# A ring of five equal x tiles, one more block loaded over GpSimd's queue, and left-over rows cut by fields, in a pairwise bilinear kernel

## Chip, cores and metric

One core of one Trainium2 chip. The metric is the device time of one execution, in microseconds. Times of a kernel are medians of its runs in the fast state; on one core the runs of one kernel here agree within about 0.3%. The profile's own span is some 1.8 us shorter than the timed run that it was taken from.

## The reference

For each of 4096 rows there are 32 fields of 64 values. For each of the 496 pairs i < j, field i is multiplied by that pair's 64 x 64 matrix, and the product is multiplied elementwise by field j. All is float32. The output has 4096 x 496 x 64 values, 520 MB; inputs are 34 MB of x and 8 MB of W.

```python
idx_i, idx_j = np.triu_indices(F, k=1)
vi = inputs[:, idx_i, :]
vj = inputs[:, idx_j, :]
vidots = jnp.einsum('bpd,pde->bpe', vi, W)
return vidots * vj
```

## The kernel before

The rows are cut into 16 blocks of 256, each of two tiles of 128 partitions, so 32 tiles of work of some 40 us each. W stays in SBUF. Per tile, PE (TensorE) transposes x and multiplies it with W, and VectorE (DVE in the views; with ACT, which is ScalarE, and GpSimd for some products) multiplies by field j into one of three output buffers. Each tile is written in four stores of about 4 MB, all from SyncE's queue.

Blocks 0 and 1 are loaded at the start. The others come in pairs, in seven **events**: at step 4 of the last tile of a pair, the next pair is loaded. The even block goes over ACT's queue, the odd one over GpSimd's, in a special shape: 120 rows, a tiny transfer, then the 8 rows that are left. The 120 rows leave one of the 16 DMA engines out. The tiny transfers are meant to keep that engine the same from event to event. The records don't show how; what was measured is that other row counts in two such transfers, before the first event and after the last, cost 30 us (1359.92 us, "Another engine left out").

```python
xb = const.tile([P, 5 * FD + 3 * GAP], F32, tag="xb", name="xb")
...
starts = [0, FD + GAP, 2 * FD + GAP, 3 * FD + GAP, 4 * FD + 2 * GAP]

def slot_of(blk: int):
    e, second = divmod(blk, 2)
    return ((1, 3), (2, 0))[e % 2][second]
...
SWR = 120

def turn_engines(k: int):
    n = k if k > 1 else 17
    c = used[0] % 8
    used[0] += 1
    src = x[: NB * n].rearrange("(p k) f d -> p k f d", k=NB)
    tc.keep_in_program_order(
        nc.gpsimd.dma_start(out=scratch[:n, :, c : c + 1], in_=src[:, :, 0, 0:1])
    )

def load_fifteen(blk: int):
    rows = rows_of(x, blk).rearrange("(p k) f d -> p k f d", k=NB)
    dst = x_block(blk)

    def part(ps: slice, ks: slice):
        tc.keep_in_program_order(nc.gpsimd.dma_start(out=dst[ps, ks], in_=rows[ps, ks]))

    part(slice(0, SWR), slice(0, NB))
    turn_engines(1)
    for k in range(NB):
        part(slice(SWR, P), slice(k, k + 1))
...
LATE = 4
loads = {place[2 * NB * e - 1, LATE]: 2 * e for e in range(1, NBLK // 2)}
...
turn_engines(5)              # before the loop over the steps
for s, (t, st) in enumerate(sched):
    if s in loads:
        load_fifteen(loads[s] + 1)
    if s - 3 in loads:
        tc.keep_in_program_order(load_x(loads[s - 3], nc.scalar))
    ...                      # transposes, two matmuls, the product
    if pa + m in ends:       # a group of pairs is complete
        nc.sync.dma_start(out=..., in_=ot[...])
turn_engines(11)             # after the loop
```

The gap in the x buffer keeps the two halves of GpSimd's blocks apart, so that they move in 8 KB packets (1792 of 8192 bytes on q0, by the packet records) rather than merged ones of 16 KB, as ACT's blocks do, which lie together (896 of 16,384 bytes on q10).

## Time and profile before

| what | value |
|---|---|
| time, median of 3 runs | 1334.1 us (1333.88 to 1335.71) |
| bytes moved, mean rate | 563 MB, 422 GB/s |
| DMA packet time, four queues | 99.3% of 16 engines' span |
| PE, VectorE busy | 86%, 71% |
| lone DMA engine at the end | about 7 us |

The four queues in the page are q1 (SyncE's: stores and first loads), q0 (GpSimd's), q10 (ACT's) and q8 (instructions). A digit in the row "DMA" says how busy the 16 engines were in a slice of the span, in tenths, and the row GB/s below it says what they moved. The two differ when packets are slow: an engine counts as busy while a packet is under way, however long it takes (1122 to 1130 us in the changed kernel: share 0.99 at 252 GB/s). The prediction shows the lines.

### The profile page before, as it was taken

How to read it: one execution, taken by the hardware profiler on the slowest of the kernel's cores; microseconds unless marked ns; L12 is line 12 of the kernel's file. 1: busy time of each engine (PE TensorE's matmuls, PEld its weight loads, DVE VectorE, ACT ScalarE, POOL GpSimd, SP SyncE). 2: the span in 40 equal slices, each digit the busy share in tenths (PEclk: the TensorE clock that was granted, in tenths of full speed). 3: DMA queues.
4: the chain of work that ended last, by engine and by line, in shares of the span. 5: the costliest groups of instructions: out<-in, count | busy, mean ns of one | idle time of the engine just before them, and what ended most of it. 6: DMA issues, size and time to landing. Idle time of an engine off the chain costs nothing.

```text
span 1333.2 us, 17377 instructions
## 1 busy us (share of the span) xinstructions
PE 1146.3 (86%) x6644; PEld 597.9 (45%) x6644; DVE 952.0 (71%) x1287; ACT 471.6 (35%) x627; POOL 558.5 (42%) x264
## 2 busy tenths in 40 slices
PE   6989989996989979998888888888888988888983
PEld 3555444443444434444444444444444444444441
DVE  5778767875777757777667776777767776677773
ACT  4553423333333323333233332343333332333330
POOL 1862524435434434344344352444434444334440
PEclk9999989998999989999899998999989999899997
DMA  9999999999999999999999999999999999999997
GB/s 389 431 430 429 381 428 433 429 433 422 428 431 434 426 423 431 430 431 428 420 435 428 434 411 426 428 433 430 422 425 437 424 430 403 428 433 430 424 426 307
DMA packets 24306, 563.16 MB, mean 422 GB/s; under 512 B 3232, under 2 KB 3232, under 8 KB 3360
## 3 DMA queue, kind: packets, MB, share of 16 engines
q1 hardware_dynamic: 20576, 532.69, 93.5%
q0 software_dynamic: 2640, 14.70, 2.8%
q10 hardware_dynamic: 1008, 14.68, 2.8%
q8 instruction: 52, 0.85, 0.2%
q14 instruction: 30, 0.25, 0.0%
HBM read 41.94 MB, written 520.09 MB: 422 GB/s over the span
## 4 chain that ended last, share of the span: by engine, by line
DMA 48%; PE 25%; DVE 11%; issue 8%; POOL 4%; ACT 3%; DVEq 0%; SPq 0%; ACTq 0%; POOLq 0%
DMA out_dram<-ob 47%; PE ps L298 22%; DVE ob L314 11%; POOL ob L312 3%; ACT ob L311 2%; PE ptx L200 2%; DMA xb<-in_r_inputs_dram 1%; PE ptw L191 1%; POOL xb L152 0%; DVE ob L181 0%; POOL scratch L144 0%; POOL ob L181 0%; DVEq L314 0%; ACT xtb L202 0%; ACT xtb L204 0%
## 5 line engine op out<-in xcount | busy, mean ns | idle before, releaser
L314 DVE TENSOR_TENSOR ob<-ps,xb 128x1024 f32<-128x1024 f32 (+4 forms) x1277 | 939.8, 793 | 347.9 <-DMA out_dram<-ob 173.8
L298 PE MATMUL ps<-wT,xtb 64*128 64x512 f32 (+15 forms) x5760 | 1015.4, 490 | 145.9 <-DVE ob L314 72.5
L312 POOL TENSOR_TENSOR ob<-ob,xb 128x1024 f32<-128x1024 f32 x224 | 529.1, 2367 | 744.6 <-ACT ob L311 717.3
L298 PEld LDWEIGHTS ps<-wT,xtb 64*128 64x128 f32 x5760 | 507.6, 195 | 619.2 <-DVE ob L314 257.1
L311 ACT COPY ob<-ps 128x1024 f32<-128x1024 f32 x224 | 226.8, 1013 | 485.9 <-PE ps L298 342.5
L202 ACT COPY xtb<-ptx 128x512 f32<-128x512 f32 x122 | 71.5, 586 | 311.4 <-PE ptx L200 309.7
L200 PE MATMUL ptx<-ident,xb 128*128 128x128 f32 x512 | 86.2, 292 | 10.8 <-DMA xb<-in_r_inputs_dram 7.1
L200 PEld LDWEIGHTS ptx<-ident,xb 128*128 128x128 f32 x512 | 55.1, 144 | 61.9 <-issue 37.5
L204 ACT COPY xtb<-ptx 64x512 f32<-64x512 f32 x122 | 71.0, 582 | 3.0
L203 ACT COPY xtb<-ptx 64x512 f32<-64x512 f32 x122 | 70.4, 577 | 2.9
L298 PE MATMUL ps<-wT,xb 64*128 64x512 f32 (+15 forms) x244 | 42.5, 465 | 3.4 <-DVE ob L314 1.6
L298 PEld LDWEIGHTS ps<-wT,xb 64*128 64x128 f32 x244 | 20.2, 185 | 21.3 <-DVE ob L314 9.4
L191 PE MATMUL ptw<-ident,ob 128*128 128x128 f32 (+1 forms) x128 | 18.1, 294 | 6.0 <-DVE ob L181 5.8
L191 PEld LDWEIGHTS ptw<-ident,ob 128*128 128x128 f32 (+1 forms) x128 | 15.1, 154 | 12.0 <-DVE ob L181 5.2
L192 ACT COPY wT<-ptw 128x1024 f32<-128x1024 f32 (+1 forms) x15 | 14.9, 992 | 10.1 <-PE ptw L191 10.0
L181 DVE COPY ob<-wT 128x1024 f32<-128x1024 f32 (+1 forms) x7 | 9.5, 1382 | 10.5 <-DMA wT<-in_L_rec_W_dram 10.5
L152 POOL DMA_DIRECT2D xb<-in_r_inputs_dram x21 | 13.3, 636 | 0.0
L202 ACT COPY xb<-ptx 128x512 f32<-128x512 f32 x6 | 3.5, 586 | 18.1 <-PE ptx L200 18.1
L144 POOL DMA_DIRECT2D scratch<-in_r_inputs_dram x9 | 8.4, 934 | 0.3 <-issue 0.3
L181 POOL COPY ob<-wT 128x1024 f32<-128x1024 f32 x4 | 8.0, 2004 | 0.0
L181 ACT COPY ob<-ob 128x1024 f32<-128x1024 f32 x2 | 4.1, 2028 | 0.0
L204 ACT COPY xb<-ptx 64x512 f32<-64x512 f32 x6 | 3.5, 583 | 0.1
(11 smaller groups left out, 11.3 us busy)
## 6 DMA issues: line engine op xcount, KB each, us to landing
out_dram<-ob SPq DMA_DIRECT2D x29, 4064.0 KB, 19.5
out_dram<-ob SPq DMA_DIRECT2D x29, 4032.0 KB, 19.9
out_dram<-ob SPq DMA_DIRECT2D x29, 4000.0 KB, 19.8
out_dram<-ob SPq DMA_DIRECT2D x29, 3776.0 KB, 20.2
xb<-in_r_inputs_dram ACTq DMA_DIRECT2D x7, 2048.0 KB, 22.5
xb<-in_r_inputs_dram POOLq DMA_DIRECT2D x7, 1920.0 KB, 33.7
out_dram<-ob SPq DMA_DIRECT2D x3, 2912.0 KB, 12.6
out_dram<-ob SPq DMA_DIRECT2D x3, 2624.0 KB, 11.2
```

Of the source, the lines that this page charges most:

```text
L152: tc.keep_in_program_order(nc.gpsimd.dma_start(out=dst[ps, ks], in_=rows[ps, ks]))
L181: ins = copy(rp[:r], src[:, k * EU : (k + 1) * EU])
L191: nc.tensor.transpose(pt[:, n, :r], rp[:r, n].rearrange("p h d -> p (h d)"), ident[:r, :r])
L192: copy(wT[:, a:b, k * EU : (k + 1) * EU], pt[:, :, :r].rearrange("p e r -> p r e"))
L200: nc.tensor.transpose(pt[:, u, :], x_tile(t)[:, f : f + 2, :].rearrange("p f d -> p (f d)"), ident)
L202: copy(xT[:, 0], pt)
L203: copy(xT[D:, 1], pt[:D])
L204: copy(xT[:D, 1], pt[D:])
L298: nc.tensor.matmul(ps[:, h, :m, :], xT[t, i // RUN][h * D : (h + 1) * D, (i + h) % 2, i % RUN // 2, :], wT[h * D : (h + 1) * D, pa : pa + ...
L311: nc.scalar.copy(dst, src)
L312: nc.gpsimd.tensor_mul(dst, dst, xj)
L314: nc.vector.tensor_mul(dst, src, xj)
```

## The change

Its intent is to take work away from the one DMA engine that is late. In the last event both blocks go over GpSimd's queue, whose large transfers leave one engine out. For that, any two tiles of the ring must be able to hold a block and still not be neighbours; so the gaps go, the ring has five equal tiles, and a table says which two of them a block takes. The 8 left rows of a block are cut into halves of the fields, each over both tiles, instead of tile by tile. The whole diff:

```diff
--- before.py
+++ after.py
@@ -68,8 +68,7 @@
 
     wT = const.tile([P, NP, E2], F32, tag="wT", name="wT")
     FD = F * D
-    GAP = 16
-    xb = const.tile([P, 5 * FD + 3 * GAP], F32, tag="xb", name="xb")
+    xb = const.tile([P, 5, FD], F32, tag="xb", name="xb")
     XT = 2 * (RUN // 2) * P
     xtb = const.tile([P, 2 * XT], F32, tag="xtb", name="xtb")
     ob = const.tile([P, 3 * cap1, D], F32, tag="ob", name="ob")
@@ -92,29 +91,34 @@
         n = xt_used[0]
         xt_used[0] += 1
         n = n % 4 if t < LEAD else n % 2
-        mem, o = (xtb, n * XT) if n < 2 else (xb, (n - 2) * XT)
+        mem, o = (xtb, n * XT) if n < 2 else (xb[:, 0], (n - 2) * XT)
         return mem[:, o : o + XT].rearrange("p (s u b) -> p s u b", s=2, b=P)
 
 
 
 
 
-    starts = [0, FD + GAP, 2 * FD + GAP, 3 * FD + GAP, 4 * FD + 2 * GAP]
-
-    def slot_of(blk: int):
+    fifteen = (3, 5, 7, 9, 11, 13, 14, 15)
+
+    def slots_of(blk: int):
         e, second = divmod(blk, 2)
-        return ((1, 3), (2, 0))[e % 2][second]
+        if e == 0:
+            return ((1, 2), (3, 4))[second]
+        if e % 2 == 0:
+            return ((2, 3), (1, 4))[second]
+        if 2 * e in fifteen:
+            return ((1, 3), (2, 0))[second]
+        return ((1, 2), (3, 0))[second]
 
     def tile_of(t: int):
 
         blk, k = divmod(t, NB)
-        return blk, 1 - k if slot_of(blk) == 0 else k
+        a, b = slots_of(blk)
+        return blk, k if a < b else 1 - k
 
     def x_block(blk: int):
-        o = starts[slot_of(blk)]
-        step = starts[slot_of(blk) + 1] - o
-        wide = xb[:, o : o + NB * step].rearrange("p (k n) -> p k n", k=NB)
-        return wide[:, :, :FD].rearrange("p k (f d) -> p k f d", d=D)
+        a, b = sorted(slots_of(blk))
+        return xb[:, a : b + 1 : b - a].rearrange("p k (f d) -> p k f d", d=D)
 
     def x_tile(t: int):
         blk, k = tile_of(t)
@@ -148,13 +152,13 @@
         rows = rows_of(x, blk).rearrange("(p k) f d -> p k f d", k=NB)
         dst = x_block(blk)
 
-        def part(ps: slice, ks: slice):
-            tc.keep_in_program_order(nc.gpsimd.dma_start(out=dst[ps, ks], in_=rows[ps, ks]))
-
-        part(slice(0, SWR), slice(0, NB))
+        def part(ps: slice, fs: slice):
+            tc.keep_in_program_order(nc.gpsimd.dma_start(out=dst[ps, :, fs], in_=rows[ps, :, fs]))
+
+        part(slice(0, SWR), slice(0, F))
         turn_engines(1)
-        for k in range(NB):
-            part(slice(SWR, P), slice(k, k + 1))
+        for h in range(2):
+            part(slice(SWR, P), slice(h * F // 2, (h + 1) * F // 2))
 
 
 
@@ -275,8 +279,10 @@
         blk, kt = tile_of(t)
         g, i, c0, m = steps[t][st]
         if s in loads:
-            load_fifteen(loads[s] + 1)
-        if s - 3 in loads:
+            for b in (loads[s], loads[s] + 1):
+                if b in fifteen:
+                    load_fifteen(b)
+        if s - 3 in loads and loads[s - 3] not in fifteen:
             tc.keep_in_program_order(load_x(loads[s - 3], nc.scalar))
         for what, *args in due.get(s, ()):
             if what == "x":
```

## The prediction

> **What bounds the kernel now.** I read the page first, then the DMA view, then windows at the end of the span, then the timeline around the last load. The page's slices of the span, its GB/s row, and three queue rows:
>
> ```profile
> DMA  9999999999999999999999999999999999999997
> GB/s 389 431 430 429 381 428 433 429 433 422 428 431 434 426 423 431 430 431 428 420 435 428 434 411 426 428 433 430 422 425 437 424 430 403 428 433 430 424 426 307
> ...
> q1 hardware_dynamic: 20576, 532.69, 93.5%
> q0 software_dynamic: 2640, 14.70, 2.8%
> q10 hardware_dynamic: 1008, 14.68, 2.8%
> q8 instruction: 52, 0.85, 0.2%
> ```
>
> The 16 DMA engines are busy in every slice but the last, at some 430 GB/s. The queues' shares (93.5, 2.8, 2.8, 0.2) add to 99.3% of 1333.2 us. PE is busy 86% and DVE 71%: compute is close behind, but DMA sets the time. So the time is one engine's packet time plus what engines idle at either end. The end is uneven. From the windows there (columns: span, length, busy time of PE, PEld, DVE, ACT, POOL, clock, DMA share, GB/s):
>
> ```profile
> 1312.00:1322.00 10.00, 0.31 (x4) 0.20 (x4) 0.77 (x4) 0.00 (x0) 0.00 (x0) 0.68 0.98 420
> 1322.00:1324.00 2.00, 0.00 (x0) 0.00 (x0) 0.00 (x0) 0.00 (x0) 0.00 (x0) 0.50 0.75 323
> 1324.00:1326.00 2.00, 0.00 (x0) 0.00 (x0) 0.00 (x0) 0.00 (x0) 0.00 (x0) 0.50 0.08 32
> 1326.00:1328.00 2.00, 0.00 (x0) 0.00 (x0) 0.00 (x0) 0.00 (x0) 0.00 (x0) 0.50 0.04 16
> ```
>
> And the DMA view of 1325.5 to 1331.5:
>
> ```profile
> DMA packets 5, 0.16 MB, mean 27 GB/s; under 512 B 0, under 2 KB 0, under 8 KB 0
> ```
>
> 27 GB/s is one sixteenth of 432. Fifteen engines are done at about 1324 to 1325 and **one engine works alone** for some 7 us, on five stores' packets of 1.19 us each. The trace's packet records show how it got there. In each 4 MB store (128 packets, eight per engine) I took the end of the last packet less that of the ninth from last: a measure of how late the slowest engine is. It is 1.1 to 2 us up to 450 us, 6.2 us just before the last load at 1116 us, 4.1 to 5.2 us just after it, and 7.0 us at the end. It grows steadily between loads and falls after each.
>
> [...] the instruction queue has 52 packets for 0.85 MB, 16 KB each. If they go to one engine, they are 52 x 0.61 us (a 16 KB packet's median) = 32 us more for it, which is what makes one engine late. [...] 1920 KB from GpSimd's queue land in 33.7 us, 2048 KB from ACT's in 22.5 us, since the former's packets are 8 KB and the latter's 16 KB, each waiting for one store packet of some 32 KB. [...] The best slices reach 433 to 437, so there is no rate to gain, only evenness.
>
> **The change part by part.**
> *Tiles.* Five equal tiles without gaps. GpSimd's blocks sit in two tiles that aren't neighbours, so their packets stay 8 KB and don't merge to 16; ACT's and the first two blocks' lie in neighbours. The order view has 1647 PE rows and 1287 DVE rows on both sides, with the same shapes. Which tile is still in use when the loads are issued (the last one of the pair before) is the same. Cost: 0. The second block's packets at the start get 16 KB instead of 8 KB: 128 packets fewer / 16 engines x some 8 ns = 0.06 us.
> *Eight left rows.* In each event 16 packets of 8 KB become 32 of 4 KB. The engines that carry them get the same bytes and one turn more: one store packet, 1.2 us later landing, one fixed cost of about 8 ns. In events 1 to 6 this block is used only after the ACT block of the same event, two tiles (80 us) later. Cost: 0.
> *Last event.* Block 14 goes from ACT's queue (16 engines) to GpSimd's (15 plus the left rows). The late engine loses eight 16 KB packets: 8 x 0.611 us at the median, 8 x 0.669 us at their mean in the trace, so 4.9 to 5.4 us. It gets 8 KB of the left rows back: 0.33 us, estimated from the 8 KB packet's 0.309 us. **Net -4.6 to -5.0 us.** The other 15 get 16 x 0.309 + 0.33 = 5.27 us in place of 8 x 0.611 = 4.89: +0.4 us.
> So the late engine, done at 1331.7 us, would be done at 1327.0, and the others, done at about 1325, at 1325.4. The lone tail shrinks from 7 us to about 2 us, and it is still what sets the end.
>
> Sum: 1334.1 - 4.6 = 1329.5 us.
>
> **The rivals.**
> *Block 14 comes late.* Alone on GpSimd's path it is slower. Before, ACT's load was issued at 1116.5 and landed at 1139; PE's first transpose of block 14 came at 1153.2 in the timeline. Now 16 packets per engine take turns with store packets: (1.2 + 0.31) x 16 = 24 us from about 1121.5, so 1146; then small packets, completion writes and left rows, some 5 to 7 us (before, 1150.3 to 1156.0). So it lands at about 1151 to 1153. Stores no longer share with ACT's load, so compute is there a few us sooner, at about 1149. A wait of 0 to 4 us on PE is likely. Against a loss: stores are issued about 9 us before the queue needs them (4 MB at 430 GB/s take 9.7 us; landing takes 19.5), so the engines don't run dry. If I misjudged that, it costs 1 to 3 us, on the relieved engine first: 1331 to 1333.
> *GpSimd's issuing delays a store.* Each block costs its sequence 0.83 + 1.01 + 1.07 = 2.9 us. One more block delays the product behind it, and the store at 1121.8, by 3 us. While stores pause, the 15 engines have the load's packets, and the late engine still has its backlog of over 6 us. Cost: 0 to 0.5 us.
> *The left-out engine isn't the late one.* Then the late one gains nothing and gets 0.4 us more: 1334.5. The falls of lateness after loads speak against it.
> *Nothing on the end after all, because the late engine idles once it is early.* It enters the event some 6 us late and is given 9.5 us over two blocks, so it could be up to 3 us early; two stores are queued, so it has work. Small.
>
> **How range and chances follow.** Mean 1329.5. Repeat runs span 1.8 us; load events lose 1 to 3.3 us to slowed packets, by chance, which moves the sum by about 1 us. If the late engine also drops the extra slowness of ACT's packets, 1328. A starved store gives 1331 to 1333. Range 1327.2 to 1333.0. A change over 2% would be 27 us: nothing in the profile is of that size, short of a mistake in the waits, and the order view shows none that is new in kind.
>
> **What would show each step.** Right: the last windows show one engine alone for 2 to 3 us rather than 7; GpSimd's queue carries 8 blocks (16.8 MB) and ACT's 6 (12.6 MB); queue shares otherwise alike; at most one short PE wait on the transfer of x near 1150 us. Wrong: DMA share falling below 0.95 between 1110 and 1190 us; a PE wait above 8 us there; a lone tail still near 7 us. The prediction fails if the tail stays, or if block 14's late landing starves the stores.

## The result

The changed kernel takes 1330.41 us (median of 4 runs, 1329.24 to 1330.74), beside 1334.9 us for the kernel before in the same rounds (4 runs). The ratio is 0.9963, interval 0.9946 to 0.9981. A ratio is the mean time of one kernel's fast runs over the mean of the other's fast runs of the same rounds, so it isn't quite the ratio of the medians. The two later rounds of five runs gave 1330.15 and 1330.02 us with ratios 0.9956 and 0.9953. The gain is about 0.4%: small, and outside the noise. The prediction was 1329.5 us.

The page of the changed kernel, the lines that answer to those shown of before (slices and GB/s, then queues with packets, MB and share of 16 engines' span):

```profile
DMA  9999999999999999999999999999999999999999
GB/s 390 430 429 426 382 431 431 431 431 422 432 430 433 429 416 431 434 429 426 420 433 431 429 422 422 433 429 430 415 425 432 431 424 383 418 430 431 433 431 389
...
q1 hardware_dynamic: 20448, 532.69, 93.8%
q0 software_dynamic: 3264, 16.80, 3.4%
q10 hardware_dynamic: 864, 12.58, 2.4%
q8 instruction: 52, 0.85, 0.2%
```

The last slice now counts as 9 and moves 389 GB/s, not 307. One block (2.1 MB) went from q10 to q0, as planned. But slice 34 fell from 403 to 383 GB/s: that is the last event, and the price of the change. By the packet records of these four queues, an engine's mean packet time rose from 1324.6 us to 1327.7 us (the page's shares are rounded, and give it only to 1 or 2 us), while the span fell by 4.7 us: the change didn't save DMA work, it removed idle time.

The end of the span, in windows (columns as in the prediction):

```profile
1322.00:1324.00 2.00, 0.00 (x0) 0.00 (x0) 0.00 (x0) 0.00 (x0) 0.00 (x0) 0.50 0.97 419
1324.00:1326.00 2.00, 0.00 (x0) 0.00 (x0) 0.00 (x0) 0.00 (x0) 0.00 (x0) 0.50 0.67 290
1326.00:1328.00 2.00, 0.00 (x0) 0.00 (x0) 0.00 (x0) 0.00 (x0) 0.00 (x0) 0.50 0.00 0
```

The share goes from 0.97 to 0 within 4 us. No engine is left alone. The DMA packet records say the same of each store (the end of its last packet less that of the ninth from last, us):

| store that ends near | before | changed |
|---|---|---|
| 1119 to 1120 us | 6.2 | 6.1 |
| 1141 to 1147 us (first after the last loads) | 5.2 | 0.5 |
| 1175 to 1177 us | 4.4 | 0.7 |
| 1232 to 1235 us | 6.2 | 1.2 |
| last store | 7.0 | 1.2 |

A packet of a store takes 1.2 us, so 1.2 is as even as it gets. In the changed kernel some engine begins each store about 5 us ahead of the others' end of the store before (1175 to 1195 us), and that lead shrinks to 1 us by the end.

The records don't name engines, but the late one can be told by its packets. An engine's packets follow each other closely, and in the kernel before those of the last engine can be followed back from the end: from 1159.4 to 1331.7 us they are 142 store packets, each starting within 8 ns of the end of the one before. They are 2 to 4% longer than those of the other engines (means from 1159 us on):

| bytes of a packet | late engine, before | the others, before | leading engine, changed | the others, changed |
|---|---|---|---|---|
| 30,208 | 1.166 us | 1.120 us | 1.156 us | 1.121 us |
| 32,000 | 1.237 us | 1.193 us | 1.234 us | 1.188 us |

Within 2 us of the last instruction of the compute engines (1312.8 us before, 1309.4 us changed) they become as short as anyone's, so a look at the lone tail doesn't show it. In the changed kernel it is the leading engine that has the long packets (followed from 1178.9 us, with gaps of at most 11 ns), so it is taken for the formerly late one. It is done at 1324.9 us. The engine that ends last, at 1327.0 us, has packets like the rest.

Now the stretch in which the last loads begin, of the kernel before and then of the changed one:

```profile
1122.00:1130.00 8.00, 7.11 (x32) 3.77 (x34) 5.78 (x7) 1.59 (x2) 3.43 (x2) 0.79 0.95 359
```

```profile
1122.00:1130.00 8.00, 8.00 (x42) 4.35 (x42) 5.59 (x7) 1.01 (x1) 6.67 (x3) 0.81 0.99 252
```

The engines are busy (0.99), but move 252 GB/s. The DMA view of these 8 us in the changed kernel says with what:

```profile
q0 software_dynamic: 205, 1.61, 86.5%
q1 hardware_dynamic: 28, 0.39, 11.5%
```

GpSimd's load has the engines nearly to itself. Its packets of 8 KB, 0.309 us elsewhere, have a median of 0.62 us among the event's first 200. A store was issued at 1124.0 us and its first packet came at 1129.6.

### The profile page after: what moved, and what is told of

Read it like the earlier page. It is cut to its first block, busy times and chain, and to the rows that moved or that the text cites.

```text
span 1328.5 us, 17383 instructions
## 1 busy us (share of the span) xinstructions
PE 1144.5 (86%) x6644; PEld 597.2 (45%) x6644; DVE 951.9 (72%) x1287; ACT 471.4 (35%) x627; POOL 560.4 (42%) x268
## 4 chain that ended last, share of the span: by engine, by line
DMA 49%; PE 21%; DVE 10%; issue 10%; POOL 5%; ACT 3%; DVEq 0%; ACTq 0%; POOLq 0%; SPq 0%
DMA out_dram<-ob 48%; PE ps L304 19%; DVE ob L320 10%; POOL ob L318 4%; ACT ob L317 2%; PE ptx L204 2%; POOL xb L156 1%; PE ptw L195 0%; DMA xb<-in_r_inputs_dram 0%; POOL ob L185 0%; POOL scratch L148 0%; DVEq L320 0%; ACT xtb L206 0%; ACT xtb L208 0%; ACT xtb L207 0%
```

## The experiments

All outputs are right. Where an edit is shown, it is against the changed kernel.

### The yardstick: the changed kernel again, twice

No edit.

> The changed kernel once more, as the yardstick on this chip. Both theories: 1330.4 +- 1 us, 4.0 to 5.0 us under the kernel before; all 16 DMA engines end within some 1.5 us, and the 10 us in which the last load begins run at 260 to 270 GB/s.

> The changed kernel once more, as the yardstick of these rounds: 1330.2 +- 1 us, 5.0 +- 1.5 us under the kernel before.

Measured: 1330.15 us (5 runs, 1329.0 to 1330.76), 5.7 us under the mean of the kernel before; in the later rounds 1330.02 us. The times are as expected. The gain over before is 5.7 and 6.4 us between means here, since the kernel before ran at 1335.9 and 1336.2 us; for the first, 4.0 to 5.0 had been expected. And 1120 to 1130 us ran at 282 GB/s in the first, not at 260 to 270. Comparisons below are with the yardstick of the same rounds where there is one.

### The third part undone: block 14 on ACT's queue

```diff
-    fifteen = (3, 5, 7, 9, 11, 13, 14, 15)
+    fifteen = (3, 5, 7, 9, 11, 13, 15)
```

> The change without its third part: block 14 is loaded on ACT's queue again (7 blocks on GpSimd's, 7 on ACT's); tiles and halves stay as changed. Theory (all of the gain comes from taking 128 KB from one late DMA engine in the last event): as the kernel before, 1334.5 +- 1.2 us, and one engine again alone at the end for 6 to 8 us at 27 GB/s. Rival (the tiles without gaps or the halves of fields give some of it): 1330 to 1333 us with a shorter tail.

Measured: 1333.85 us, ratio 0.9990 (0.9976 to 1.0004) to before, where the yardstick has 0.9956 (0.9944 to 0.9968). The means differ by 1334.33 - 1330.05 = 4.3 us. The windows at its end:

```profile
1322.00:1324.00 2.00, 0.00 (x0) 0.00 (x0) 0.00 (x0) 0.00 (x0) 0.00 (x0) 0.50 0.30 129
1324.00:1330.00 6.00, 0.00 (x0) 0.00 (x0) 0.00 (x0) 0.00 (x0) 0.00 (x0) 0.50 0.05 22
```

One engine is alone again for 6 us (22 to 27 GB/s, a sixteenth of the whole). So the third part carries the gain. With tiles and halves alone the means differ from before by 1.4 us, and the interval takes in no difference.

### The second part undone: left rows tile by tile

```diff
-        def part(ps: slice, fs: slice):
-            ...out=dst[ps, :, fs], in_=rows[ps, :, fs]...
-        part(slice(0, SWR), slice(0, F))
+        def part(ps: slice, ks: slice):
+            ...out=dst[ps, ks], in_=rows[ps, ks]...
+        part(slice(0, SWR), slice(0, NB))
         turn_engines(1)
-        for h in range(2):
-            part(slice(SWR, P), slice(h * F // 2, (h + 1) * F // 2))
+        for k in range(NB):
+            part(slice(SWR, P), slice(k, k + 1))
```

> The change without its second part: the 8 left rows go tile by tile again (16 packets of 8 KB in place of 32 of 4 KB per event). Theory (the halves cost and give nothing): 1330.4 +- 1 us, same tail as the changed kernel. Rival (the doubled turns of the left rows cost time in the eight events): 0.5 to 1.5 us less.

Measured: 1330.87 us, ratio 0.9966 (0.9953 to 0.9978) to before. The interval overlaps the yardstick's widely, so no effect was found; the rival, that undoing it gains, is not supported.

### Another engine left out

The first small transfer gets 6 rows instead of 5 and the last 10 instead of 11. This is meant to leave another engine out of the large transfers; all else is the same.

```diff
-    turn_engines(5)
+    turn_engines(6)
...
-    turn_engines(11)
+    turn_engines(10)
```

> The changed kernel [...] (6 rows instead of 5 in the first small transfer, 10 instead of 11 in the last): [...] all else is the same. Theory (what counts is that the engine left out is the one that also carries the instruction refills): that engine now has 8 x 4.9 us of load packets more, so about 39 us more in all, and the time is 1360 to 1372 us, with the lateness of one engine growing until stores wait for it. Rival (any engine left out would do, or the gain comes from elsewhere): 1330 to 1334 us.

Measured (one run): 1359.92 us, 30 us over the yardstick and 24 us over the one run of the kernel before beside it. Its end:

```profile
1348.00:1350.00 2.00, 0.00 (x0) 0.00 (x0) 0.00 (x0) 0.00 (x0) 0.00 (x0) 0.50 0.08 32
1350.00:1356.00 6.00, 0.00 (x0) 0.00 (x0) 0.00 (x0) 0.00 (x0) 0.00 (x0) 0.50 0.06 27
```

Only the two row counts differ, so the 30 us are put down to which engine is left out, though the records name none; the rival is refuted. The size was expected at 39 us, 8 blocks x 4.9 us; it is 30, six blocks' worth. The records suggest why: from 160 to 450 us no engine is late by more than about 2 us in the kernel before (2.6 us at 150 us), so part of the relief in the first events fell where it wasn't needed. A later experiment bears on that.

### The cost of loads by themselves

Behind the last stores, four more loads of one block, one after another; longer on purpose (one run, 1368.99 us), with the same outputs. The lines that define the views `wide`, `flat` and `rows` are cut here.

```diff
+    ...
+    for eng, n, dst in (
+        (nc.gpsimd, SWR, wide),      # 120 rows, 8 KB packets
+        (nc.gpsimd, P, wide),        # 128 rows, 8 KB
+        (nc.scalar, P, wide),        # 128 rows, 8 KB
+        (nc.scalar, P, flat),        # 128 rows, 16 KB
+    ):
+        tc.keep_in_program_order(eng.dma_start(out=dst[:n], in_=rows[:n]))
+    turn_engines(1)
     turn_engines(11)
```

> Measures a disputed cost by itself; longer on purpose. Behind the last stores the changed kernel loads one block four times more, one load after another: 120 rows on GpSimd's queue, 128 rows on GpSimd's, 128 rows on ACT's, all three in 8 KB packets, and 128 rows on ACT's in 16 KB packets. Theory [...]: the first moves about 200 GB/s with packets of some 0.5 us, the other three over 380 GB/s with packets of 0.31 and 0.61 us. Rival A (reads of x are slow whatever the shape): all four 200 to 260 GB/s. Rival B (GpSimd's path is slow): the first two slow, ACT's two fast.

The DMA view has (KB each, us from issue to landing):

```profile
ob<-in_r_inputs_dram ACTq DMA_DIRECT2D x2, 2048.0 KB, 8.1
ob<-in_r_inputs_dram POOLq DMA_DIRECT2D x1, 2048.0 KB, 8.8
ob<-in_r_inputs_dram POOLq DMA_DIRECT2D x1, 1920.0 KB, 12.6
```

The smaller load takes longer. By the packet records, from first to last packet, the four moved 191, 302, 325 and 313 GB/s, with median packets of 0.641, 0.309, 0.309 and 0.611 us. So it is neither x nor GpSimd's path that is slow, but the 15-engine shape when it runs alone; rivals A and B fall. The last three are below the 380 GB/s that was expected: the engines weren't busy throughout (DMA share 0.82, 0.79 and 0.69 in windows of 6 to 6.5 us about them).

Why 15 engines are slow stays open. Of the 240 packets of the 120 rows, 17 took 0.33 us or less. All 17 begin within 0.9 us (1330.06 to 1330.94 us), so they belong to many engines: one engine's 16 in a row would take 5 us. Which engine wrote which rows isn't recorded.

### The same block on 16 engines

```diff
+        if blk == 14:
+            part(slice(0, P), slice(0, F))
+            return
         part(slice(0, SWR), slice(0, F))
```

> The changed kernel, but block 14 goes over GpSimd's queue in one transfer of 128 rows, on 16 engines, so the late engine is not relieved of it. Theory: the time goes back to 1333 to 1335 us with one engine alone at the end for 5 us or more; and the stretch of the load alone at the last event is half as long, its packets 0.31 to 0.4 us instead of 0.5 to 0.65, since 15 engines with eight rows each are what makes them slow. Rival A (moving the block to GpSimd's queue is what helps, whichever engines): 1330.2 +- 1. Rival B (the load alone is slow on 16 engines too, for it reads HBM while other things go on): stretch and packets as with 120 rows.

Measured: 1332.74 us (4 runs), ratio 0.9974 (0.996 to 0.9987). First the stretch of the last event, then the end:

```profile
1122.00:1130.00 8.00, 8.00 (x40) 4.26 (x38) 5.57 (x7) 1.01 (x1) 4.50 (x2) 0.79 0.99 395
```

```profile
1322.00:1324.00 2.00, 0.00 (x0) 0.00 (x0) 0.00 (x0) 0.00 (x0) 0.00 (x0) 0.50 0.12 48
1324.00:1330.00 6.00, 0.00 (x0) 0.00 (x0) 0.00 (x0) 0.00 (x0) 0.00 (x0) 0.50 0.06 27
```

The stretch moves 395 GB/s instead of 252, and the first 200 packets have a median of 0.309 us: the slow stretch belongs to 15 engines, in place too. And one engine is alone for over 6 us again, with the late engine's long packets (1.238 us for 32,000 bytes): only leaving that engine out takes the tail away. The times alone say less. This version is still faster than the kernel before, its interval overlaps slightly with those of the yardsticks (0.9953 and 0.9956, from other rounds) and with that of block 14 on ACT's queue (0.9990), so that GpSimd's queue as such gives a part is not ruled out. Fifteen engines are done about 2.8 us sooner than in the changed kernel's first profile (the ninth from last packet at 1323.0 rather than 1325.8 us), and the kernel is slower. The time was 0.3 us under the low edge of the expectation.

### Block 15 issued later

```diff
-            for b in (loads[s], loads[s] + 1):
-                if b in fifteen:
-                    load_fifteen(b)
+            if loads[s] in fifteen:
+                load_fifteen(loads[s])
+            else:
+                load_fifteen(loads[s] + 1)
+        if s - 4 in loads and loads[s - 4] in fifteen:
+            load_fifteen(loads[s - 4] + 1)
```

> In the last event block 15's load is issued four steps later, behind GpSimd's product of the first group, so that 2.9 us of issuing no longer stand before that product and its store. Theory (the other 15 engines end 1.5 us later than predicted since that store came 2.8 us later and the load's packets alone moved only some 200 GB/s meanwhile): the first store of that tile is issued near 1121.3 us rather than 1124.0, the slow stretch at 1122 to 1130 us shrinks to a few us, the 15 engines end 1 to 2 us sooner; the time falls by 0 to 1.5 us, as the formerly late engine still ends at about 1327. Rival (the load's packets hold the engines however early the store is issued): stretch and time unchanged, 1330.4 +- 1.

Measured: 1331.41 us, ratio 0.9968 (0.9955 to 0.998). My theory was wrong. The store was issued at 1122.9 us, 11.1 us behind the one before it rather than 13.8, so the delay was indeed gone; yet its first packet came at 1128.8, and the stretch was no better:

```profile
1122.00:1130.00 8.00, 7.35 (x34) 3.86 (x36) 5.84 (x7) 1.90 (x2) 7.23 (x7) 0.79 0.98 262
```

In the five profiles with this event (changed kernel, its two repeats, left rows by tile, and this one) the store's ninth packet began 6.1 to 6.3 us after its issue, where 1.0 to 1.3 us is usual in the kernel before with little ahead of it (stores issued at 1092 to 1111 us). But the kernel before had most of this delay too: 5.4 us for its store issued at 1121.8 us, 5.5 us with block 14 back on ACT's queue, and 4.3 us with block 14 on 16 engines. So it isn't peculiar to two blocks on GpSimd's queue. It did not wait for the load to be through: when the store's first packet began, some 190 of the load's packets had begun in three of the five, 162 in another and 111 here. Nor did it wait for the late engine's previous store, which here ended at 1131.4, after the new one had begun. What holds it stays open. In this profile, which is of the slowest of the five runs, the formerly late engine is also last again, 3.3 us behind the others at the end (1329.9 and 1326.6 us).

### Nine blocks

Blocks 12 and 13 both on GpSimd's queue as well, with a row in the table of tiles for an even event.

```diff
-    fifteen = (3, 5, 7, 9, 11, 13, 14, 15)
+    fifteen = (3, 5, 7, 9, 11, 12, 13, 14, 15)
...
+        if e % 2 == 0 and 2 * e in fifteen:
+            return ((1, 3), (2, 4))[second]
         if e % 2 == 0:
```

> One dose more: event 6 also has both of its blocks (12 and 13) on GpSimd's queue, so 9 blocks leave the late engine out instead of 8. Theory (with 8 the engines already end together, and each such event costs the other 15 engines 0.4 us of left rows and some 2 us in which a load on 15 engines runs alone): no further gain, 1330 to 1333 us, and the formerly late engine is done some 3 to 5 us ahead of the others. Rival (the late engine still sets the end, as the prediction said): 1326 to 1328.5 us.

Measured: 1330.22 us, ratio 0.9956 (0.9943 to 0.9968) beside the yardstick's 0.9953 (0.994 to 0.9967). No further gain, as the theory said. It was wrong on the end, though: no engine is done ahead. At 1324 to 1326 us one is still alone, at 16 GB/s. By its packets this is not the formerly late one: those of 32,000 bytes mostly take 1.185 us, as anyone's.

### The same dose in the middle

The same table row, and block 8 (event 4) instead of block 14 (event 7).

```diff
-    fifteen = (3, 5, 7, 9, 11, 13, 14, 15)
+    fifteen = (3, 5, 7, 8, 9, 11, 13, 15)
```

> The same dose at another place: block 8 in event 4, in the middle of the run, goes to GpSimd's queue in place of block 14 in event 7. Theory (the sum of the late engine's packets counts, and what an event costs depends on whether a store is queued when the load comes; in the middle the lateness is 3 us rather than 6 and stores are issued 4 us before the engines need them rather than 1): the engines end together again, the stretch in which the load runs alone is shorter or gone, 1328.0 to 1330.0 us. Rival (the place doesn't matter, or the lateness must be taken away near the end): 1330.2 us or more.

Measured: 1331.91 us, ratio 0.9964 (0.9952 to 0.9977). This misses the expected gain, and isn't clearly slower. Its end:

```profile
1322.00:1324.00 2.00, 0.00 (x0) 0.00 (x0) 0.00 (x0) 0.00 (x0) 0.00 (x0) 0.50 0.30 129
1324.00:1328.00 4.00, 0.00 (x0) 0.00 (x0) 0.00 (x0) 0.00 (x0) 0.00 (x0) 0.50 0.06 24
```

The late engine is alone for 4 to 5 us, as if most of the relief had been lost. The records fit: before event 4 it was 4.2 us late, afterwards 1.5 to 2.3, and no engine then led by more than the usual 1 to 2 us, whereas the same dose in event 7 turned 6.1 us late into a lead of 5. My reading, not shown by itself, is that an engine that has caught up gets ahead only if a store is queued for it. That relief counts only where there is a backlog is thus supported, and it is the same shortfall as in the experiment with another engine; the loss itself wasn't seen packet by packet.

### Loads at step 8

```diff
-    LATE = 4
+    LATE = 8
```

> The changed kernel with every event's loads issued at step 8 of their tile instead of step 4, behind GpSimd's product of the first group: the loads then reach the engines with a fresh store queued. Theory (the loads cost time where they run alone, at some 190 GB/s on 15 engines): the slowed-packet time of the events falls, by 1.5 to 5 us over all seven, so 1325.5 to 1329 us, and no stretch under 300 GB/s at the last event. Rival (the slowed packets come from reading and writing at once): 1330.2 +- 1.

Measured: 1331.59 us, ratio 0.9969 (0.9956 to 0.9981): no gain. Half of the theory held:

```profile
1122.00:1130.00 8.00, 6.75 (x38) 3.72 (x34) 4.83 (x7) 1.53 (x2) 5.98 (x5) 0.86 1.01 423
```

No slow stretch is left there. But the wait view of 1130 to 1200 us has a new line (engine, line, what it waited for: us, times, longest):

```profile
PE ptx L204 <- DMA xb<-in_r_inputs_dram: 6.3, 1, 6.3
```

PE stood 6.3 us for block 14, which the prediction had feared at step 4. The store behind it was issued at 1158.2, 19.2 us after the one before, and the leading engine's lead fell from 3 us to nothing.

### Ten blocks

Blocks 8, 12 and 14.

```diff
-    fifteen = (3, 5, 7, 9, 11, 13, 14, 15)
+    fifteen = (3, 5, 7, 8, 9, 11, 12, 13, 14, 15)
```

> The last dose: blocks 8, 12 and 14, so three events, have both of their blocks on GpSimd's queue (10 blocks there, 4 on ACT's). Theory (relief counts only where the late engine has a backlog; with 9 the fifteen were done at 1323 us and the late one 2 us later): the lone engine at the end is gone, the others end at 1323 to 1325 us, 1328 to 1331 us in all, so not clearly under the 1330.0 of the changed kernel. Rival (each dose still gives): 1325 to 1328 us.

Measured: 1333.56 us, ratio 0.9981 (0.9968 to 0.9995), above the expected range and, by the ratios, slower than eight blocks (0.9953 and 0.9956). One engine was still alone for some 3 us at the end, which I had expected gone; its packets of 32,000 bytes take 1.185 us, so it too isn't the formerly late one. Seven blocks: 1333.85; eight: 1330.15 and 1330.02; nine: 1330.22; ten: 1333.56. No version tried beats the changed kernel clearly.

## Why the prediction was right, point by point

The time came out as predicted, 1329.5 and 1330.4 us. Of the steps, one was right (one late engine that gains from being left out), the reason given for its lateness was wrong, and two sizes were off in opposite directions, so that the sum fits in part by luck.

- **The bound.** Right. The end is set by the slowest DMA engine. Taking 2.1 MB off 16 engines and putting it on 15 changes the time by 4.3 us, with the same bytes (block 14 back on ACT's queue), and where all 16 engines carry it over GpSimd's queue the lone tail is back. That there is no rate to gain is an estimate from the slices (best 433 to 437 GB/s, mean 422).
- **Which engine.** Right: with the engine left out changed, by two row counts, the kernel takes 30 us more. That it is the same engine in each event was assumed, not shown; in the last one the records agree: beside the 15 load packets under way at a time, one engine still works on a store that ends 6.1 us late.
- **Why it is late.** Wrong: the instruction refills aren't on that engine, as far as it can be followed. Six refills begin between 1159 and 1332 us in the kernel before, and its 142 packets leave no room for one: each refill begins in the middle of one of them. Nor is there room in the changed kernel (1178.9 to 1305.5 us, six refills). The refills go elsewhere: 39 of the 44 after 200 us begin 3 to 4 ns before a store packet ends, as one engine's packets follow each other, where about 3% would do so by chance. A refill also takes longer than the prediction took it to, 0.94 us at the median and not 0.61. What the records show of this engine instead is store packets that are 2 to 4% longer. An estimate from the kernel before: 0.035 us on each of eight packets in 116 stores of about 4 MB are some 32 us over the run, by chance what the prediction gave the refills. Why they are longer, and only while the compute engines run, stays open; that the recording of the profile plays a part isn't ruled out.
- **-4.6 to -5.0 us on the late engine.** Too small: its last packet was predicted at 1327.0 us and came at 1324.9, so it gained 6.8 us. What the 2 us beyond the prediction are wasn't taken apart. That the last packet of all came at 1327.0 us, as predicted for the late engine, is luck: it is another engine's. Undoing the part measured 4.3 us.
- **The others +0.4 us, and a lone tail of 2 us.** The others' ninth-from-last packet came at 1325.8 and 1324.6 us in two profiles, beside 1324.7 before: +1.1 and -0.1. The tail is one packet, 1.2 us, and no longer the late engine's: it is the others that set the end, in place of "it is still what sets the end". Here the sum left out a term: at the last event the load ran alone on 15 engines, its packets taking twice as long. Slowed-packet time in that event (what packets took over size / 27.2 GB/s + 9 ns, which fits the median packets, per engine) rose from 2.0 to 4.9 us, and 4.1 in the repeat. With the predicted 0.4 us this would be 2.5 to 3.3 us at the end; that less came of it must be less idle time elsewhere, which wasn't measured.
- **Tiles and left rows cost nothing.** Nothing was found. Together, without the third part, their interval takes in no difference to before; undoing the left rows' cut alone can't be told from the yardstick. The tiles weren't tried by themselves. The fixed cost of some 8 ns a packet fits the medians: 2 x 0.309 - 0.611 = 0.007 us.
- **Rival: block 14 comes late.** The predicted wait of 0 to 4 us did not occur. The step that failed is 24 us for sixteen turns with store packets. Such turns are in the records (before, from 300 us on: of 507 packets of ACT's loads that begin within 12 ns of the end of just one other packet, 427 follow a store's, 75 one of GpSimd's and 5 one of their own queue's). But no stores came between 1123.5 and 1129.6 us, so there were no turns to take, and the 120 rows landed 23.5 us after issue, at 1139.4, not at 1146. The wait is real at step 8: 6.3 us.
- **Rival: GpSimd's issuing delays a store.** The delay was right (13.8 us between the two stores' issues, not 11.1), its cost was not: it was put at 0 to 0.5 us because "the 15 engines have the load's packets", which took twice as long (0.62 us, not 0.309). But taking the delay away brought nothing, since the store then waited all the same.
- **Rival: the relieved engine idles.** Not in event 7, where it took a lead of 5 to 6 us and not of the 3 us that were reckoned. It is what seems to have happened with block 8 in event 4.

## What to carry to other kernels

When DMA is the bound, look at how the engines end, not only at the mean rate: a windows view whose share falls to a sixteenth (0.06, 27 GB/s) is one engine alone, and its length bounds roughly what balance can give (here 7 us, of which 4.3 were gained). Before giving a reason for its lateness, follow its packets back and compare their lengths with the others': here the reason given, a queue with the right number of packets, was not on that engine wherever it could be followed. Relieve it where it has a backlog: relief given to an engine that was on time seems to have been lost here (block 8: 1331.91 us beside 1330.02). And read GB/s beside the busy share: a load on 15 engines counted as 0.99 busy while moving 252 GB/s.
